# Layer 3 self attention: two norms by single units, and a gate projection in another place

## Chip, cores and metric

The kernel runs on one core of a Trainium2 chip. The metric is the device time of one execution in microseconds (us). A core has five engines that matter here: PE (TensorE, matrix products and transposes), DVE (VectorE), ACT (ScalarE), POOL (GpSimd) and SP, which issues most DMAs. Each engine works through its own queue in order, and engines wait for one another through semaphores.

## What is computed

The program is a network of four layers on 1024 tokens (16 sequences of 64) of 256 channels. The change lies in the self attention of the last layer, a linear attention with convolutions over the sequence around it. Its reference, cut:

```python
x = x + _dwconv(x.transpose(0, 2, 1), cpe1_w, cpe1_b).transpose(0, 2, 1)
shortcut = x
xn = _ln(x, norm1_g, norm1_b)
act_res = silu(xn @ actp_w + actp_b)
xi = xn @ in_w + in_b
xi = silu(_dwconv(xi.transpose(0, 2, 1), dwc_w, dwc_b)).transpose(0, 2, 1)
qk = xi @ qk_w + qk_b
q = elu(qk[..., :c]) + 1.0
k = elu(qk[..., c:]) + 1.0
...
attn = attn + _dwconv(v_bcl, lepe_w, lepe_b).transpose(0, 2, 1)
x = shortcut + attn * act_res @ out_w + out_b
x = x + _dwconv(x.transpose(0, 2, 1), cpe2_w, cpe2_b).transpose(0, 2, 1)
xn2 = _ln(x, norm2_g, norm2_b)
mlp = gelu(xn2 @ fc1_w + fc1_b, approximate=False) @ fc2_w + fc2_b
return x + mlp
```

`_dwconv` is a convolution of three taps along the sequence, one set of taps per channel. `_ln` subtracts the mean over the channels and divides by the root of the variance plus 1e-5, then applies a gain and an offset. `act_res` is called the gate here.

## The kernel before

The method `L3_attn` works on four units (NU) of 256 tokens each. Most tiles are 128 partitions by two halves by 256 elements; a unit lies either feature by token (channels on the partitions, in two halves) or token by feature ("natural"). All eight PSUM banks belong to one pool, `ps`: every matrix product or turn of a unit takes one bank, and a bank is free again when its last reader is done. SBUF tiles come from a pool with four buffers for each tag (`a` to `f`), so that a tag that is used again waits for the readers of what it held.

Instructions that are wrapped in `pin` (and all matrix products and turns, L195 and L199) keep the order of the code on their engine. What isn't wrapped, such as POOL's operations and the builds of the diagonal matrices (L1738), may be placed by the scheduler.

The stages, each a loop over the four units that ends before the next begins:

1. The input is turned to feature by token (L199) and copied by ACT (L1893). `conv` then makes the first convolution: half of the channels on PE as three products with diagonal matrices (`conv_T`) and an evacuation by ACT that adds the bias (L1905), the other half on DVE as three operations (`conv_V`, L1754, L1755 and L1758), here called the taps.
2. `norm`: each unit is turned to natural, `measure` finds mean and variance on DVE (L1813, L1814) and adds 1e-5 (L1816), POOL takes the power -0.5 (L1817), and `normal` subtracts the mean and multiplies on DVE (L1822), one unit behind the measuring.
3. The normalised units are turned back and scaled by gain and offset on ACT (L1829).
4. For each unit, the input projection (bias by DVE, L1919) and then the gate projection (Silu by ACT, L1836, kept in tag `d`).
5. The second convolution with Silu (L1926, L1929).
6. Queries, keys and values: two projections and a turn per unit on PE, exponentials on ACT, elu on DVE (L1939, L1944, L1953), and a third convolution on DVE alone (lepe, six operations of `conv_V`).
7. `products`, `attend` and `gated`, staggered by one unit each: products of keys and values, masked on DVE (L1982, L1986); the attention (L2006 to L2008); the turn back, the sum with lepe (L2020) and the product with the gate on POOL (L2021).
8. The output projection with bias and shortcut on DVE (L2035), for all units; then the third convolution for all units; then `norm` again, which here also adds each natural unit to the residual `x` on DVE (L2049) right after its measuring.
9. Turn, scale, and the two layers of the MLP (`hidden` with Gelu on ACT, L2062, and `output`). The experts of the next stage follow.

An activation function of ACT that isn't in the loaded table set needs a table load first; the trace shows one ahead of the exponentials of stage 6 and one ahead of the Gelus of stage 9.

Of the kernel before, what the change touches and what calls it, by code (L numbers as in the profile page):

```python
# [8 lines left out]
F32 = mybir.dt.float32  # L9
U8 = mybir.dt.uint8  # L10
U32 = mybir.dt.uint32
AF = mybir.ActivationFunctionType
ALU = mybir.AluOpType
# [3 lines left out]
P = 128  # L17
# [156 lines left out]
class Net:  # L174
# [33 lines left out]
    def pv(self, name):  # L208
        o, n = self.pat[name]
        return self.pvec[:, o : o + n]  # L210
# [1529 lines left out]
    def conv_T(self, ps, src, dg):  # L1740


        o = ps.rearrange("p (b s) -> p b s", s=S)
        i = src.rearrange("p (b s) -> p b s", s=S)
        self.mm(o, dg[:, 1, :], i, True, False)
        self.mm(o[:, :, 1:], dg[:, 0, :], i[:, :, : S - 1], False, False)
        self.mm(o[:, :, : S - 1], dg[:, 2, :], i[:, :, 1:], False, True)

    def conv_V(self, out, src, taps, b):

        nc = self.nc
        o = out.rearrange("p (b s) -> p b s", s=S)
        i = src.rearrange("p (b s) -> p b s", s=S)
        self.pinned(nc.vector.tensor_scalar(o, i, taps[1], b, ALU.mult, ALU.add))  # L1754
        self.pinned(nc.vector.scalar_tensor_tensor(  # L1755
            o[:, :, 1:], i[:, :, : S - 1], taps[0], o[:, :, 1:], ALU.mult, ALU.add
        ))
        self.pinned(nc.vector.scalar_tensor_tensor(  # L1758
            o[:, :, : S - 1], i[:, :, 1:], taps[2], o[:, :, : S - 1], ALU.mult, ALU.add
        ))  # L1760
# [4 lines left out]
    def L3_attn(self, w):  # L1765
# [3 lines left out]
        nc, tc = self.nc, self.tc  # L1769
        in_w, actp_w, qk_w, out_w = w  # L1770
        pv = lambda n: self.pv(f"L3_attn_{n}")
        NH, NU, U = 8, 4, 256
        pin = self.pinned
# [4 lines left out]
        with (  # L1778
# [5 lines left out]
            def T(tag):  # L1784
                return wk.tile([P, 2, U], F32, tag=tag, name=tag)
# [4 lines left out]
            def turned(src, at):  # L1790

                ps = bank()
                for i in range(2):
                    for kc in range(2):
                        self.tr(ps[:, i, kc * P : (kc + 1) * P], at(src, i, kc))
                return ps
# [4 lines left out]
            def project(w, src, c0=0):  # L1801
                ps = bank()
                for c in range(2):
                    cols = slice(c0 + c * P, c0 + (c + 1) * P)
                    self.project_T(ps[:, c, :], w, src, cols, slice(None))
                return ps

            def measure(ps):

                mv = small.tile([P, 2, 2], F32, tag="mv", name="mv")  # L1810
                for i in range(2):
                    st = small.tile([P, 6], F32, tag="bst", name="bst")
                    pin(nc.vector.bn_stats(st, ps[:, i, :]))  # L1813
                    pin(nc.vector.bn_aggr(mv[:, i, :], st))  # L1814
                rs = small.tile([P, 2], F32, tag="rs", name="rs")
                pin(nc.vector.tensor_scalar(rs, mv[:, :, 1], 1e-5, None, ALU.add))  # L1816
                nc.gpsimd.tensor_tensor(rs, rs, self.c("pow")[:, 0:1].to_broadcast([P, 2]), ALU.pow)  # L1817
                return ps, mv, rs

            def normal(out, ps, mv, rs):  # L1820
                for i in range(2):
                    pin(nc.vector.tensor_scalar(  # L1822
                        out[:, i, :], ps[:, i, :], mv[:, i, 0:1], rs[:, i : i + 1],
                        ALU.subtract, ALU.mult,
                    ))

            def scaled(out, ps, g, b):
# [6 lines left out]
            def biased(out, ps, fn, b):  # L1834
                for c in range(2):
                    pin(nc.scalar.activation(  # L1836
                        out[:, c, :], ps[:, c, :], fn, bias=b[:, c : c + 1]
                    ))

            def norm(xT, tag, extra=None):  # L1840


                out, due = [], None
                for u in range(NU + 1):
                    now = None
                    if u < NU:
                        ps = turned(xT[u], to_nat)
                        now = measure(ps)
                        if extra is not None:
                            extra(u, ps)  # L1850
                    if due is not None:
                        n = wk.tile([P, 2, U], F32, tag=tag, name=tag)
                        normal(n, *due)
                        out.append(n)
                    due = now
                return out

            self.fixed = True
# [33 lines left out]
                x0T.append(T("a"))  # L1892
                pin(nc.scalar.copy(x0T[u], ps))  # L1893
            self.add_bias(8)
            def conv(out, src, n):
                ps = self.psum(pp, [P, U], "ps")
                self.conv_T(ps, src[:, 0, :], dg[n])
                self.conv_V(out[:, 1, :], src[:, 1, :], taps[n][1], pv(f"{n}_b")[:, 1:2])
                return ps

            x1T = []
            for u in range(NU):
                x1T.append(T("c"))
                ps = conv(x1T[u], x0T[u], "cpe1")
                pin(nc.scalar.activation(  # L1905
                    x1T[u][:, 0, :], ps, AF.Identity, bias=pv("cpe1_b")[:, 0:1]
                ))
            self.diagonals(dg["dwc"], taps["dwc"][0])
            self.diagonals(dg["cpe2"], taps["cpe2"][0])
            n1 = norm(x1T, "a")  # L1910
            xnT = []
            for u in range(NU):
                xnT.append(T("b"))
                scaled(xnT[u], turned(n1[u], to_feat), pv("norm1_g"), pv("norm1_b"))
            act, xi0 = [], []
            for u in range(NU):
                ps = project(in_w, xnT[u])
                xi0.append(T("a"))
                pin(nc.vector.tensor_tensor(xi0[u], ps, wide(pv("in_b")), ALU.add))  # L1919
                act.append(T("d"))  # L1920
                biased(act[u], project(actp_w, xnT[u]), AF.Silu, pv("actp_b"))
            xi = []
            for u in range(NU):
                xi.append(T("e"))
                ps = conv(xi[u], xi0[u], "dwc")
                pin(nc.scalar.activation(  # L1926
                    xi[u][:, 0, :], ps, AF.Silu, bias=pv("dwc_b")[:, 0:1]
                ))
                pin(nc.scalar.activation(xi[u][:, 1, :], xi[u][:, 1, :], AF.Silu))  # L1929

            qT, k, v, lepe = [], [], [], []
            for u in range(NU):
                ps = project(qk_w, xi[u])
                e = sp.tile([P, 2, U], F32, tag="e", name="e")
                biased(e, ps, AF.Exp, pv("qk_b"))
                z = sp.tile([P, 2, U], F32, tag="z", name="z")
                biased(z, ps, AF.Identity, qb1)
                qT.append(T("b"))
                pin(nc.vector.scalar_tensor_tensor(qT[u], e, 1.0, z, ALU.min, ALU.max))  # L1939
                ps = bank()  # L1940
                for i in range(2):
                    self.project_N(ps[:, i, :], xi[u], i, qk_w, slice(D, 2 * D))
                z = sp.tile([P, 2, U], F32, tag="zk", name="zk")
                pin(nc.vector.tensor_tensor(  # L1944
                    z, ps, kb1.unsqueeze(1).to_broadcast([P, 2, D]), ALU.add
                ))
                e = sp.tile([P, 2, U], F32, tag="e", name="e")
                pin(nc.scalar.activation(e, z, AF.Exp, bias=self.c("neg1")))
                ps = turned(xi[u], to_nat)
                v.append(T("a"))  # L1950
                pin(nc.scalar.copy(v[u], ps))
                k.append(T("f"))
                pin(nc.vector.scalar_tensor_tensor(k[u], e, 1.0, z, ALU.min, ALU.max))  # L1953

                lepe.append(self.xn[:, 2 * u : 2 * u + 2, :])
                for c in range(2):
                    self.conv_V(
                        lepe[u][:, c, :], xi[u][:, c, :], taps["lepe"][c],
                        pv("lepe_b")[:, c : c + 1],
                    )  # L1960

            kvm = {}

            def products(u):
# [58 lines left out]
            for n in range(NU + 2):  # L2023
# [3 lines left out]
                    attend(n - 1)  # L2027
                if 0 <= n - 2 < NU:
                    gated(n - 2)
            x2T = []  # L2030
            for u in range(NU):
                ps = project(out_w, y[u])
                x2T.append(T("a"))
                for c in range(2):
# [1 line left out]
                        x2T[u][:, c, :], ps[:, c, :], pv("out_b")[:, c : c + 1], x1T[u][:, c, :],  # L2036
                        ALU.add, ALU.add,
                    ))
            x3T = []
            for u in range(NU):  # L2040
                x3T.append(T("b"))
                ps = conv(x3T[u], x2T[u], "cpe2")
                pin(nc.scalar.activation(
                    x3T[u][:, 0, :], ps, AF.Identity, bias=pv("cpe2_b")[:, 0:1]
                ))

            def add(u, ps):
                xu = self.x[:, 2 * u : 2 * u + 2, :]
                pin(nc.vector.tensor_tensor(xu, ps, xu, ALU.add))  # L2049

            n2 = norm(x3T, "a", add)
            xn2T, hT = [], {}
            for u in range(NU):
                xn2T.append(T("c"))
# [77 lines left out]
```

## Time and profile before

| | |
|---|---|
| median of 3 runs | 3475.49 us (3474.08 to 3479.93) |
| profiled execution | 3481.06 us, span 3479.3 us |
| mean granted PE clock in it | 0.942 of full speed |
| L3_attn, first convolution to the first expert rows | about 3102 to 3257 us of the span |

The profile is one execution as the hardware profiler saw it. Engine rows give busy time; the timeline merges runs of equal instructions and names in brackets how long the engine was idle before, and which engine's instruction ended that. The clock of PE is what the throttle granted, as a share of full speed. A matrix product of 32-bit numbers stands in the trace as two instructions, so 32 instructions are the four products of each of four units. The ends of PE's instructions are modelled, so that starts are the safer reading.

### The profile page before, as it was taken

The numbers are of one execution on the slowest core, as the hardware profiler recorded it, in microseconds if no ns is written. First come the engines' busy times: TensorE is split into PE (matmuls) and PEld (weight loads), VectorE is DVE, ScalarE is ACT, GpSimd is POOL, SyncE is SP. The second block draws the span as 40 slices with busy tenths as digits, with TensorE's granted clock in tenths as the row PEclk, the third lists the DMA queues.
The fourth block names the chain that finished last, engine by engine and source line by source line (L and its number), as shares of the span: only waits on it lengthen the run. The fifth ranks groups of instructions, "written<-read, shape, count | busy, mean of one in ns | idle before, by whom it ended". The sixth has DMA issues, their size and how long they took to land.

```text
span 3479.3 us, 69200 instructions
## 1 busy us (share of the span) xinstructions
PE 3170.8 (91%) x29623; PEld 2365.5 (68%) x29623; DVE 1387.8 (40%) x3702; ACT 1065.1 (31%) x2191; POOL 470.1 (14%) x478
## 2 busy tenths in 40 slices
PE   7999998699899999999998689999987978888798
PEld 4666664499566666666665367777766966767697
DVE  6888885622333333333334862222234010126300
ACT  3555654111112111212111112222221367753111
POOL 2333222222100000000000000000001311110132
PEclk9999998699899999999998699999997979998899
DMA  6333331389011112111139001111114835520297
GB/s 198 103 126 124 94 115 58 122 289 320 17 58 56 57 57 76 38 60 55 57 113 308 15 13 57 57 57 57 38 53 162 273 123 179 187 88 1 107 324 246
DMA packets 178368, 395.12 MB, mean 114 GB/s; under 512 B 11446, under 2 KB 142270, under 8 KB 165214
## 3 DMA queue, kind: packets, MB, share of 16 engines
q1 hardware_dynamic: 165070, 372.81, 31.2%
q0 software_dynamic: 11712, 16.00, 2.3%
q8 instruction: 234, 3.83, 0.5%
q10 hardware_dynamic: 1280, 1.89, 0.2%
q14 instruction: 72, 0.59, 0.1%
HBM read 374.94 MB, written 16.12 MB: 112 GB/s over the span
## 4 chain that ended last, share of the span: by engine, by line
PE 77%; DVE 11%; DMA 5%; issue 5%; POOL 1%; ACT 1%; SPq 0%; POOLq 0%; ACTq 0%; DVEq 0%
PE acc L195 16%; PE pss L195 15%; PE pst L195 13%; PE pst L199 9%; PE pso L195 5%; PE psk L195 5%; PE s L195 4%; PE p L195 4%; DMA l3o<-y,token 3%; PE ps L195 3%; PE psh L195 2%; DVE Sx L447 2%; DVE Sx L470 1%; POOL rs L304 1%; PE py L195 1%
## 5 line engine op out<-in xcount | busy, mean ns | idle before, releaser
L199 PE MATMUL pst<-cst,Sx 128*128 128x128 f32 (+1 forms) x2568 | 377.7, 286 | 42.9 <-DVE Sx L470 14.1
L195 PE MATMUL pss<-ctxT,qk 128*128 128x512 f32 (+1 forms) x1024 | 403.3, 519 | 0.0
L199 PEld LDWEIGHTS pst<-cst,Sx 128*128 128x128 f32 (+1 forms) x2568 | 287.9, 144 | 167.0 <-issue 70.2
L195 PE MATMUL acc<-ctx,PT 128*128 128x256 f32 (+1 forms) x1664 | 374.0, 382 | 0.0
L195 PEld LDWEIGHTS acc<-ctx,PT 128*128 128x128 f32 (+1 forms) x1664 | 314.1, 192 | 40.2
L447 DVE CUSTOM_DVE_ANT_0 Sx<-s,mneg 128x384 f32<-128x384 f32 (+1 forms) x512 | 262.7, 567 | 79.0 <-PE s L195 69.8
L304 POOL TENSOR_TENSOR rs<-rs,cst 128x1 f32<-128x1 f32 x96 | 57.4, 600 | 1602.3 <-DVE rs L303 1495.4
L491 ACT ACTIVATE PT<-pst 128x384 f32<-128x384 f32 x512 | 221.3, 489 | 154.1 <-PE pst L199 152.8
L824 ACT ACTIVATE Pr<-pss 128x512 f32<-128x512 f32 (+1 forms) x512 | 220.4, 523 | 68.8 <-PE pss L195 67.3
L376 ACT ACTIVATE Sx<-Sx,nm 128x1601 f32<-128x1601 f32 x64 | 104.4, 1631 | 432.2 <-DVE nm L630 432.2
L195 PEld LDWEIGHTS pss<-ctxT,qk 128*128 128x128 f32 x1024 | 160.9, 190 | 79.3 <-issue 72.3
L195 PE MATMUL pso<-W,hT 128*128 128x256 f32 x884 | 200.9, 379 | 0.0
L195 PE MATMUL pst<-wst,ctxT 128*128 128x256 f32 (+1 forms) x832 | 183.4, 381 | 0.0
L195 PE MATMUL psk<-ctxT,wst 128*128 128x512 f32 (+1 forms) x512 | 181.8, 513 | 0.8 <-ACT qT L686 0.8
L195 PEld LDWEIGHTS pso<-W,hT 128*128 128x128 f32 x884 | 163.3, 190 | 19.6
L195 PEld LDWEIGHTS pst<-wst,ctxT 128*128 128x128 f32 (+1 forms) x832 | 153.6, 186 | 25.8 <-issue 2.7
L195 PE MATMUL pss<-q,ctxT 32*128 32x128 f32 (+1 forms) x3328 | 151.3, 300 | 16.6 <-issue 13.9
L195 PE MATMUL s<-ctxT,q 32*128 32x384 f32 (+1 forms) x1024 | 160.2, 572 | 6.3 <-DVE mx L447 4.9
L625 DVE TENSOR_SCALAR_CACHE_REDUCE Sx<-pss 128x1024 f32<-128x1024 f32 (+1 forms) x128 | 127.0, 992 | 82.6 <-PE pss L195 82.6
L640 DVE TENSOR_SCALAR Z<-acc,rec 128x256 f32<-128x256 f32 x64 | 31.0, 484 | 322.6 <-PE acc L195 322.6
L195 PEld LDWEIGHTS pss<-q,ctxT 32*128 32x128 f32 (+1 forms) x3328 | 119.4, 194 | 48.5 <-issue 39.5
L195 PEld LDWEIGHTS psk<-ctxT,wst 128*128 128x128 f32 x512 | 88.3, 190 | 93.6 <-issue 92.0
(387 smaller groups left out, 4479.1 us busy)
## 6 DMA issues: line engine op xcount, KB each, us to landing
ctxT<-in_ctxT_dram SPq DMA_DIRECT2D x64, 1601.0 KB
ctx<-in_ctx_dram SPq DMA_DIRECT2D x48, 1536.0 KB
W<-in_L_experts_dram SPq DMA_DIRECT2D x61, 1024.0 KB
W<-in_L_experts_dram SPq DMA_DIRECT2D x23, 1536.0 KB
ctx<-in_ctx_ones_dram SPq DMA_DIRECT2D x16, 1632.0 KB
W<-in_L_experts_dram SPq DMA_DIRECT2D x23, 768.0 KB
W<-in_L_experts_dram SPq DMA_DIRECT2D x15, 1028.0 KB
m<-in_mask_dram SPq DMA_DIRECT2D x32, 100.1 KB
```

Of the source, the lines that this page charges most:

```text
L195: self.pinned(self.nc.tensor.matmul(out, lhsT, rhs, start=start, stop=stop))
L199: self.pinned(self.nc.tensor.transpose(out, in_, self.ident[:n, :n]))
L304: nc.gpsimd.tensor_tensor(rs, rs, self.c("pow")[:, 0:1], ALU.pow)
L376: nc.scalar.activation(Sx, Sx, AF.Exp, bias=bias, scale=scale, accum_out=total)
L447: self.pinned(nc.vector.tensor_tensor_reduce(out=Sx[:, j, :n], in0=ps[j][:, :n], in1=st["mneg"][:, o : o + n], op0=ALU.add, op1=ALU.max, s ...
L470: self.pinned(nc.vector.tensor_scalar(Sj[j], Sj[j], m[:, j : j + 1], None, ALU.subtract))
L491: self.pinned(nc.scalar.activation(PT, ps, AF.Exp))
L625: nc.vector.tensor_scalar(Sx[:, o : o + n], ps[:, :n], HD**-0.5, None, ALU.mult, ALU.max, accum_out=mx[:, h : h + 1],)
L640: nc.vector.tensor_scalar(Z, acc, rec, None, ALU.mult)
L824: nc.scalar.activation(st["Pr"][:kn, g : g + n, j, :], ps[j][:kn, :n, :], AF.Silu)
```

## The change

Four things change in `L3_attn`:

- `norm` gets a function that makes the convolution of one unit, and calls it unit by unit: convolve, turn and measure unit u, normalise unit u - 1. Before, all four convolutions were made ahead of it. In `first` and `third`, PE's part, DVE's part and ACT's evacuation of one unit stand together.
- `normal` runs on ACT: it computes x times the inverse deviation plus minus mean times the inverse deviation. For that, DVE negates the mean (one more operation of 128 by 2), and POOL makes one more product.
- The gate projection moves from stage 4 to a place behind stage 6; its tiles take tag `b`, the queries tag `d`.
- In stage 8, DVE's part of the third convolution follows each unit's output projection. The additions to the residual come after the whole norm, which holds the natural units' banks until then.

```diff
-                rs = small.tile([P, 2], F32, tag="rs", name="rs")
-                pin(nc.vector.tensor_scalar(rs, mv[:, :, 1], 1e-5, None, ALU.add))
-                nc.gpsimd.tensor_tensor(rs, rs, self.c("pow")[:, 0:1].to_broadcast([P, 2]), ALU.pow)
-                return ps, mv, rs
+                rs = small.tile([P, 2, 2], F32, tag="rs", name="rs")
+                pin(nc.vector.tensor_scalar(rs[:, 0, :], mv[:, :, 1], 1e-5, None, ALU.add))
+                pin(nc.vector.tensor_scalar(rs[:, 1, :], mv[:, :, 0], -1.0, None, ALU.mult))
+                nc.gpsimd.tensor_tensor(
+                    rs[:, 0, :], rs[:, 0, :], self.c("pow")[:, 0:1].to_broadcast([P, 2]), ALU.pow
+                )
+                nc.gpsimd.tensor_tensor(rs[:, 1, :], rs[:, 1, :], rs[:, 0, :], ALU.mult)
+                return ps, rs
...
-                    pin(nc.vector.tensor_scalar(
-                        out[:, i, :], ps[:, i, :], mv[:, i, 0:1], rs[:, i : i + 1],
-                        ALU.subtract, ALU.mult,
+                    pin(nc.scalar.activation(
+                        out[:, i, :], ps[:, i, :], AF.Identity, bias=rs[:, 1, i : i + 1],
+                        scale=rs[:, 0, i : i + 1],
                     ))
...
-            def norm(xT, tag, extra=None):
+            def norm(conv, tag, extra=None):
...
-                        ps = turned(xT[u], to_nat)
+                        ps = turned(conv(u), to_nat)
                         now = measure(ps)
-                        if extra is not None:
-                            extra(u, ps)
+                        nat.append(ps)
                     if due is not None:
                         n = wk.tile([P, 2, U], F32, tag=tag, name=tag)
                         normal(n, *due)
                         out.append(n)
                     due = now
+                if extra is not None:
+                    for u in range(NU):
+                        extra(u, nat[u])
...
-            for u in range(NU):
+            def first(u):
                 x1T.append(T("c"))
-                ps = conv(x1T[u], x0T[u], "cpe1")
+                ps = conv_T(x0T[u], "cpe1")
+                conv_V(x1T[u], x0T[u], "cpe1")
                 pin(nc.scalar.activation(
                     x1T[u][:, 0, :], ps, AF.Identity, bias=pv("cpe1_b")[:, 0:1]
                 ))
+                return x1T[u]
+
+            n1 = norm(first, "a")
             self.diagonals(dg["dwc"], taps["dwc"][0])
             self.diagonals(dg["cpe2"], taps["cpe2"][0])
-            n1 = norm(x1T, "a")
...
-                act.append(T("d"))
-                biased(act[u], project(actp_w, xnT[u]), AF.Silu, pv("actp_b"))
...
+            act = []
+            for u in range(NU):
+                ps = project(actp_w, xnT[u])
+                act.append(T("b"))
+                biased(act[u], ps, AF.Silu, pv("actp_b"))
             kvm = {}
...
-            x3T = []
-            for u in range(NU):
-                x3T.append(T("b"))
-                ps = conv(x3T[u], x2T[u], "cpe2")
+                x3T.append(T("d"))
+                conv_V(x3T[u], x2T[u], "cpe2")
+
+            def third(u):
+                ps = conv_T(x2T[u], "cpe2")
                 pin(nc.scalar.activation(
                     x3T[u][:, 0, :], ps, AF.Identity, bias=pv("cpe2_b")[:, 0:1]
                 ))
+                return x3T[u]
...
-            n2 = norm(x3T, "a", add)
+            n2 = norm(third, "a", add)
```

More of the change, by code (lines that the diff above doesn't have):

```diff
@@ L1814, in measure, with normal @@
                     pin(nc.vector.bn_aggr(mv[:, i, :], st))
-                rs = small.tile([P, 2], F32, tag="rs", name="rs")
-                pin(nc.vector.tensor_scalar(rs, mv[:, :, 1], 1e-5, None, ALU.add))
-                nc.gpsimd.tensor_tensor(rs, rs, self.c("pow")[:, 0:1].to_broadcast([P, 2]), ALU.pow)
-                return ps, mv, rs
-            def normal(out, ps, mv, rs):
+                rs = small.tile([P, 2, 2], F32, tag="rs", name="rs")
[6 more added lines that the diff above has]
+                return ps, rs
+            def normal(out, ps, rs):
                 for i in range(2):
-                    pin(nc.vector.tensor_scalar(
-                        out[:, i, :], ps[:, i, :], mv[:, i, 0:1], rs[:, i : i + 1],
-                        ALU.subtract, ALU.mult,
+                    pin(nc.scalar.activation(
+                        out[:, i, :], ps[:, i, :], AF.Identity, bias=rs[:, 1, i : i + 1],
+                        scale=rs[:, 0, i : i + 1],
                     ))
@@ L1838, in biased @@
                     ))
-            def norm(xT, tag, extra=None):
-                out, due = [], None
+            def norm(conv, tag, extra=None):
+                out, nat, due = [], [], None
                 for u in range(NU + 1):
@@ L1894, in L3_attn, with conv_V, conv_T @@
             self.add_bias(8)
-            def conv(out, src, n):
+            def conv_V(out, src, n):
+                self.conv_V(out[:, 1, :], src[:, 1, :], taps[n][1], pv(f"{n}_b")[:, 1:2])
+            def conv_T(src, n):
                 ps = self.psum(pp, [P, U], "ps")
                 self.conv_T(ps, src[:, 0, :], dg[n])
-                self.conv_V(out[:, 1, :], src[:, 1, :], taps[n][1], pv(f"{n}_b")[:, 1:2])
                 return ps
             x1T = []
-            for u in range(NU):
+            def first(u):
                 x1T.append(T("c"))
-                ps = conv(x1T[u], x0T[u], "cpe1")
+                ps = conv_T(x0T[u], "cpe1")
+                conv_V(x1T[u], x0T[u], "cpe1")
                 pin(nc.scalar.activation(
@@ L1914, in L3_attn @@
                 scaled(xnT[u], turned(n1[u], to_feat), pv("norm1_g"), pv("norm1_b"))
-            act, xi0 = [], []
+            xi0 = []
             for u in range(NU):
@@ L1924, in L3_attn @@
                 xi.append(T("e"))
-                ps = conv(xi[u], xi0[u], "dwc")
+                ps = conv_T(xi0[u], "dwc")
+                conv_V(xi[u], xi0[u], "dwc")
                 pin(nc.scalar.activation(
@@ L1937, in L3_attn @@
                 biased(z, ps, AF.Identity, qb1)
-                qT.append(T("b"))
+                qT.append(T("d"))
                 pin(nc.vector.scalar_tensor_tensor(qT[u], e, 1.0, z, ALU.min, ALU.max))
@@ L2029, in L3_attn @@
                     gated(n - 2)
-            x2T = []
+            x2T, x3T = [], []
             for u in range(NU):
```

## The prediction

> **What bounds the kernel now.** I read the page first, its busy times:
>
> ```profile
> PE 3170.8 (91%) x29623; PEld 2365.5 (68%) x29623; DVE 1387.8 (40%) x3702; ACT 1065.1 (31%) x2191; POOL 470.1 (14%) x478
> ```
>
> PE is by far the busiest engine, so the question in any stage is what PE waits for. The operations of the changed method lie between 3099 and 3256 us of the span, so I read the timeline of PE there, then that of VectorE (DVE) at PE's gaps, the waits, and last the stretches' granted clock. Columns of a timeline: start, length, engine, line, operation, count, and in brackets the idle time before.
>
> PE's timeline, in the order of the steps below:
>
> ```profile
> 3101.83 5.29 PE L195 MATMUL ps<-a,dgs 128*128 128x256 f32 x24
> 3106.96 1.91 PE L199 MATMUL ps<-cst,c 128*128 128x128 f32 x16
> 3110.86 0.91 PE L199 MATMUL ps<-cst,a 128*128 128x128 f32 x4 [1.99 <-DVE a L1822]
> 3113.05 1.26 PE L199 MATMUL ps<-cst,a 128*128 128x128 f32 x4 [1.28 <-DVE a L1822]
> 3115.24 2.17 PE L199 MATMUL ps<-cst,a 128*128 128x128 f32 x8 [0.93 <-DVE a L1822]
> 3117.20 15.28 PE L195 MATMUL ps<-b,wst 128*128 128x256 f32 x64
> 3132.31 5.29 PE L195 MATMUL ps<-a,dgs 128*128 128x256 f32 x24
> ...
> 3164.57 2.08 PE L195 MATMUL ps<-kvm,b 128*64 128x136 f32 x16 [7.23 <-DVE kvm L1986]
> ...
> 3195.80 1.27 PE L199 MATMUL ps<-cst,a 128*128 128x128 f32 x4 [3.76 <-DVE a L1822]
> 3198.59 1.26 PE L199 MATMUL ps<-cst,a 128*128 128x128 f32 x4 [1.52 <-DVE a L1822]
> 3201.37 2.17 PE L199 MATMUL ps<-cst,a 128*128 128x128 f32 x8 [1.52 <-DVE a L1822]
> ```
>
> PE waits three times: in the first norm (4.2 us in three pieces), before the attention (7.23), in the second norm (6.8). Each time DVE is behind. Between 3132 and 3164 the chain of waits runs through DVE and ScalarE (ACT), 5.46 us a unit, while PE runs ahead and ends at 3157.3.
>
> VectorE's timeline at both ends of that stretch, and ACT's last work there:
>
> ```profile
> 3131.40 0.40 DVE L1754 TENSOR_SCALAR e<-a,pvec 128x256 f32<-128x256 f32 x1
> ...
> 3163.10 1.28 DVE L1982 TENSOR_TENSOR kvm<-ps,cst 128x512 f32<-128x512 f32 x2
> ```
> ```profile
> 3138.43 1.28 ACT L1836 ACT_TABLE_LOAD   x1
> ...
> 3159.65 0.56 ACT L1951 COPY a<-ps 128x512 f32<-128x512 f32 x1
> ```
>
> Windows of 3.41 us (length, PE busy and count, clock granted, DMA share, GB/s):
>
> ```profile
> 3109.66:3113.07 3.41, 0.87 (x5) 0.99 0.00 0
> 3113.07:3116.49 3.42, 2.50 (x9) 0.50 0.00 0
> 3116.49:3119.90 3.41, 3.41 (x12) 0.51 0.02 5
> 3157.45:3160.86 3.41, 0.00 (x0) 0.50 0.00 0
> 3164.27:3167.69 3.42, 3.12 (x26) 0.51 0.02 5
> 3201.82:3205.23 3.41, 3.41 (x13) 0.51 0.00 0
> ```
>
> Each idle stretch costs twice: PE then works at half clock until a full window has passed. The 64 projections took 15.28 us where 32 warm ones take 7.07: 1.1 us lost.
>
> **What the Trainium skill says.** "TensorE: Matmul & The Clock Gate", Part 1, has a free-running window of 3413 ns, half clock after an idle one and full clock after a busy one. The trace agrees: all changes above fall on one grid of 3.41 us. It does not say where between idle and busy the line runs; in this trace, of fifteen full-speed windows with 52 to 60% busy, nine were followed by full and six by half speed. "PSUM — Partial Sum Buffer", Engine vs sequencer instructions, calls ScalarE's, VectorE's and GpSimd's queues strict FIFO: an ACT instruction that waits holds all behind it; in the trace ACT starts its work in the order of the code throughout the method. "ScalarE: Activation LUTs", What ACT_TABLE_LOAD costs, gives 1283 ns for a load and about 1380 for the drain; the trace shows 1.28 and no gap after it. "GPSIMD Engine Reference", Specifications, says that POOL shares SBUF interfaces with DVE: a 128x128 DVE operation took 0.75 us beside POOL's 128x256 add (3101.63), but a pair took 0.47 beside a power (3100.23), so I charge the small POOL operations nothing on DVE.
>
> **Step 1, the first norm (loss 2.5).** Before, all convolutions end on PE at 3107.12 and the projections start at 3117.41. After, unit u+1's DVE taps come behind unit u's measuring, and that waits for unit u's turn on PE, which waits for its taps. The loop on DVE: measuring 1.30 (3107.59 to 3108.89) plus 0.09 for the added TENSOR_SCALAR, taps 1.35 (a quarter of 5.4), 0.14 to PE, three turns of four at 0.15, 0.05 back: 3.38 a unit. The first measuring starts at 3101.99 + 1.28 (convolution) + 0.51 (ACT) + 0.14 + 0.60 + 0.05 = 3104.6, the fourth at 3114.7, done 3116.1. Then POOL's power 0.70 and the new product. No row shows a 128x2 product; the bounds are 0.10 (the 128x1 memsets) and 0.70 (the power); I take 0.3, since 128x256 and 128x512 products or adds (0.75 and 1.27) leave about 0.23 as fixed part. ACT's two normalising operations take 1.02 as a pair (the same form at L1829), so they end at 3118.3. The scaling of unit 0 is queued behind them on ACT, 0.56 and a wait of 0.14 for its first half: projections start at 3119.3, 2.0 later than now. PE is busy 1.9 of 3.4 us in the loop, 56%, in the doubtful band: 0.5 more, as a share of the 1.4 that half speed would cost. The six diagonal builds moved behind the norm (0.27 each) fall into DVE's waits of 0.6 a unit.
>
> **Step 2, gate projection and its ACT work leave the stretch (gain 6.1).** Now: 3117.41 to 3138.43 (ACT free for the table load), 21.0. After: 32 projections 7.07, 1.2 for a cold start as now; then DVE is last, not PE: 0.05, the last bias add 0.61, four units of taps 5.50 (3131.40 to 3136.90), 0.04, the last Silu 0.41, together 6.6 (PE's convolutions need 5.6). Sum 14.9. So the keys' stretch starts 6.1 - 2.5 = 3.6 earlier. Inside it nothing changes: DVE and ACT set the 5.46 a unit.
>
> **Step 3, the gate projection in PE's gap (0).** PE ends the keys' work 3153.1 - 3.6 = 3149.5 or before; 7.07 of projections end by 3156.5; the first products 2.2, 3158.7. The eight PSUM banks: the four gate banks are freed by ACT's Silus, which wait on ACT behind the last key's exponent and copy (3160.2 - 3.6 = 3156.6), an added table load 1.28, then 0.84 for the first unit and 0.73 each: 3158.7, 3159.5. The second products need these two banks and end at about 3161.0. The attention would wait for DVE's masks until 3164.57 - 3.6 = 3161.0 anyway. Cost 0; with the page's drain on top, 1.4. What is late next is DVE again. POOL's gating first needs a gate at 3168 or later.
>
> **Step 4, PE warm at the attention (gain 0.6).** The first 16 attention matmuls took 2.08 against 1.15 later, the next 16 products 1.64 against 1.16: 1.4 on PE. DVE, 91% busy there, idled 0.64 and 0.19 for PE; I take 0.6 of the 0.8.
>
> **Step 5, the second norm (gain 2.6).** DVE now ends its taps at 3191.44. After, each unit's 0.88 (two adds) and 1.36 (taps) go side by side with the output projections, 2.27 a unit from 3180.03: done at 3189.1. PE's loop from 3185.1: convolution 1.28, ACT 0.51, 0.14, turns 0.6. ACT's queue decides from the third unit: unit 0 is measured by 3190.5, through POOL 3191.65, normalised on ACT until 3192.7, and only behind this comes unit 2's convolution evacuation; so unit 2 is turned at 3193.85, unit 3 at 3196.35, measured 3197.8, through POOL 3199.0, normalised 3200.0, scaled behind it; the hidden layer starts at 3200.9 against 3203.54. The residual adds (0.6 each), now last on DVE, hold two PSUM banks until 3199.1, just in time. The cold start there, 0.8 now, I leave as it is. Behind it PE bounds the rest of the method, and the routing of the experts starts from its last row, so a shift carries to the end.
>
> **Sum.** -2.5 + 6.1 + 0 + 0.6 + 2.6 = 6.8 us. It is made on the execution with span 3479.3 and time 3481.06, which lies 5.6 above the median shown; the difference goes on the median: 3475.49 - 6.8 = 3468.7. Bounds of the unknowns: product -0.2/+0.4 twice, drain +1.4, clock -2 to +3.
>
> **Rivals.** (a) Half clock takes the gain back: the first loop falls to half speed (0.9 over my allowance), the projections start cold in an unlucky window (1.3 more), the second loop loses 1.2 and the hidden layer 0.9. Gain 2.5, 3473.0. For it: the 56%. Against: the second loop is 60 to 75% busy at first. (b) All stays warm and the windows fall well: 0.6 less in step 1, 1.2 saved in the projections, 0.2 more in step 4, 0.8 more at the hidden layer, and the allowance of 0.5 back: gain 10.1, 3465.4. (c) Slower: half speed from the second unit of both loops makes PE itself the loop's bound: convolution 2.57, ACT and waits 0.65, turns 1.2, so 4.4 a unit against 3.4 and 2.5. That is 2.6 over my allowance and 1.0 more at the projections in the first, 4.5 and 0.9 in the second: 9.0 lost against 6.8 gained, 3477.7. It decides when both loops go cold by their second unit; more than 0.2% needs the drain and a bank wait in step 3 as well, or a mechanism that I don't see.
>
> **How the numbers follow.** About 0.2%, 7 us, is what a measurement of this kernel can tell from no change. Chances: forecast 0.46 (3465 to 3472), (a) 0.22, (b) 0.20, (c) 0.12. Over half of the forecast's own spread and all of (b) lie at 7 us or more: faster 0.48; slower by 0.2%, most of (c) with what I overlook: 0.09; the rest 0.43. Range 3462 to 3476: it leaves out the end of (b) and (c).
>
> **What would show it.** Right: PE's 7.23 us gap gone, gate projections in it, the first 16 attention matmuls near 1.15; projections starting near 3119 with DVE as the loop's bound; one more table load; the hidden layer some 7 us earlier. Wrong: half clock through the first loop; a PE wait for ACT's Silu before the second products; PE waiting for residual adds in the second norm; the third unit's evacuation not held by the normalising.

## The result

| | before | changed |
|---|---|---|
| median of 20 runs each | 3473.98 us (3464.96 to 3484.77) | 3464.36 us (3455.90 to 3474.02) |
| profiled execution | 3481.06 us, span 3479.3 | 3462.45 us, span 3460.7 |

The changed kernel takes 0.9975 of the time before (95% interval 0.9964 to 0.9986), or 8.7 us less (4.9 to 12.5). 6.8 were forecast. The median is inside the forecast's range of 3462 to 3476, but 4.3 us under its single number of 3468.7. Of these, 1.5 come from the base: 20 runs put the kernel before at 3473.98, the three runs shown earlier at 3475.49. The interval also holds the 10.1 us of rival (b), so the times alone do not choose between the forecast and (b).

The two profiled spans differ by 18.6 us, and most of that isn't the change. The first product with a diagonal matrix, where the changed code begins, starts at 3101.83 in the one and at 3090.37 in the other: 11.5 us arise in earlier stages, whose code is the same, and I did not look for their cause. So all stage times below are counted from that product (the origin), each in its own execution:

| from the origin to, us | before | changed | difference |
|---|---|---|---|
| projections start | 15.37 | 17.02 | +1.65 |
| table load ahead of the exponentials | 36.60 | 32.58 | -4.02 |
| attention's first product | 62.74 | 58.72 | -4.02 |
| output projection | 76.20 | 72.32 | -3.88 |
| hidden layer's first product | 101.51 | 94.64 | -6.87 |
| last product of the method | 157.83 | 150.18 | -7.65 |
| end of the span | 377.47 | 370.33 | -7.14 |

The page's busy times of the changed kernel, then its PE timeline in the order of the steps:

```profile
PE 3158.9 (91%) x29623; PEld 2352.3 (68%) x29623; DVE 1381.7 (40%) x3694; ACT 1073.6 (31%) x2208; POOL 473.7 (14%) x486
```
```profile
3095.93 0.55 PE L199 MATMUL ps<-cst,c 128*128 128x128 f32 x3 [0.72 <-DVE c L1758]
...
3099.37 0.55 PE L199 MATMUL ps<-cst,c 128*128 128x128 f32 x3 [0.72 <-DVE c L1758]
...
3106.48 1.00 PE L199 MATMUL ps<-cst,a 128*128 128x128 f32 x4 [1.81 <-ACT a L1826]
3107.39 8.88 PE L195 MATMUL ps<-b,wst 128*128 128x256 f32 x32
3116.11 5.29 PE L195 MATMUL ps<-a,dgs 128*128 128x256 f32 x24
...
3136.81 7.07 PE L195 MATMUL ps<-b,wst 128*128 128x256 f32 x32
...
3146.95 1.16 PE L195 MATMUL ps<-a,f 64*128 64x128 f32 x14 [0.58 <-ACT b L1840]
3148.04 1.05 PE L195 MATMUL ps<-cst,f 128*128 128x2 f32 x8
3149.09 2.08 PE L195 MATMUL ps<-kvm,d 128*64 128x136 f32 x16
3151.11 1.77 PE L195 MATMUL ps<-a,f 64*128 64x128 f32 x16
...
3177.74 0.66 PE L199 MATMUL ps<-cst,d 128*128 128x128 f32 x4 [1.68 <-ACT d L2060]
...
3184.09 1.00 PE L199 MATMUL ps<-cst,a 128*128 128x128 f32 x4 [1.50 <-ACT a L1826]
3185.01 14.11 PE L195 MATMUL ps<-c,ctxT 128*128 128x256 f32 x64
```

The reader is to see three things. The turns of units 1 and 2 in the first norm are 3.44 us apart, each after a wait for DVE's taps. The 7.23 us gap ahead of the attention is gone: the gate projection fills it, and 0.58 of waiting for a Silu is left. But the attention's first 16 products take 2.08 us as before: the gap has gone and the slow start has not. In the second norm the turn of the third unit waits 1.68 us for ACT, where the other three wait 0.56 or 0.57.

The windows (length, PE busy and count, clock, DMA share, GB/s) of the changed kernel, laid on the changes of this execution's clock to within 0.1 us; the first is in the first norm, the next two around the start of the projections, the last two around the start of the attention:

```profile
3096.01:3099.42 3.41, 2.13 (x11) 1.00 0.00 0
3104.57:3107.98 3.41, 1.47 (x8) 1.00 0.00 0
3107.98:3111.40 3.42, 3.42 (x10) 0.51 0.00 0
3145.53:3148.94 3.41, 2.83 (x28) 1.00 0.00 0
3148.94:3152.36 3.42, 3.42 (x30) 0.51 0.00 0
```

A window with 2.13 us of busy PE keeps the clock, one with 1.47 loses it. The fourth loses it too, although PE was busy for 2.83 of its 3.41 us. That is the one thing in the trace that the prediction's picture doesn't explain, and half of the experiments turn on it.

### The profile page after: what moved, and what is told of

Read it like the earlier page. It is cut to its first block, busy times and chain, and to the rows that moved or that the text cites. A ratio compares the mean times of both kernels' runs of the same rounds, so it can differ in the third digit from the quotient of the medians.

```text
span 3460.7 us, 69219 instructions
## 1 busy us (share of the span) xinstructions
PE 3158.9 (91%) x29623; PEld 2352.3 (68%) x29623; DVE 1381.7 (40%) x3694; ACT 1073.6 (31%) x2208; POOL 473.7 (14%) x486
## 4 chain that ended last, share of the span: by engine, by line
PE 78%; DVE 12%; issue 4%; DMA 3%; POOL 1%; ACT 1%; SPq 0%; POOLq 0%; ACTq 0%; DVEq 0%
PE acc L195 16%; PE pss L195 15%; PE pst L195 13%; PE pst L199 9%; PE pso L195 6%; PE psk L195 5%; PE p L195 4%; PE s L195 4%; PE psh L195 3%; PE ps L195 2%; DVE Sx L447 2%; DMA l3o<-y,token 1%; DVE Sx L470 1%; POOL rs L304 1%; PE py L195 1%
## 5 line engine op out<-in xcount | busy, mean ns | idle before, releaser
L195 PE MATMUL pss<-q,ctxT 32*128 32x128 f32 (+1 forms) x3328 | 149.2, 296 | 16.3 <-issue 13.5
L726 DVE TENSOR_TENSOR v<-pst,bvec 128x512 f32<-128x512 f32 (+1 forms) x112 | 73.0, 652 | 196.2 <-PE pst L195 196.2
```

The source lines that it names most:

```text
L195: self.pinned(self.nc.tensor.matmul(out, lhsT, rhs, start=start, stop=stop))
L726: nc.vector.tensor_tensor(o, ps[:kn, :n, :], bv[:kn].to_broadcast([kn, n, D]), ALU.add)
```

## Experiments

My theory after the traces: the change is a sum of parts (move of the gate projection, first norm, second norm) that can be read off the marks, plus a clock effect in the attention's stage that was not understood. The rival: the parts hang together, or the clock is just noise. All kernels were profiled once and timed (6 to 22 runs) against the kernel before; ratios are to it. It was timed anew with each group of kernels, with medians of 3476.26, 3471.64 and 3476.01, so times of different groups are compared by ratios. "Marks" are four starts counted from the origin: projections, attention, output projection, hidden layer; "the stage" is the time from attention to output projection.

**The move alone.** The kernel before, with the gate projection behind the keys' work and the tags adapted:

```diff
-                act.append(T("d"))
-                biased(act[u], project(actp_w, xnT[u]), AF.Silu, pv("actp_b"))
...
+            act = []
+            for u in range(NU):
+                ps = project(actp_w, xnT[u])
+                act.append(T("b"))
+                biased(act[u], ps, AF.Silu, pv("actp_b"))
             kvm = {}
```

> The kernel before with the gate projection moved and nothing else. Marks count from the first diagonal product of the first convolution: projections start at 15.4, the attention's first product at 62.7, the output projection at 76.2, the hidden layer at 101.5 in the kernel before, and at 17.0, 58.7, 72.3 and 94.6 in the changed one. Theory (the parts add up, and this move alone shortens the way from projections to attention by 5.6): 15.4, 57.1, 70.6 and 96, so 5.5 us faster than before. Rival (the norms and the move are worth something only together, since the gap closes from both sides): less than 3 us faster.

Measured: ratio 0.9986 (0.9976 to 0.9997), 4.9 us faster. Marks 15.37, 57.10, 76.33, 101.64. The attention comes 5.64 earlier, as the theory says, and in the profiled execution all of it is lost again before the output projection: 19.2 us for a stage that took 13.5. The timeline of this stage (`cst,f` with 128x2 are the sums of the keys, two columns wide) and its windows, laid on the changes of the clock:

```profile
3153.68 1.87 PE L195 MATMUL ps<-cst,f 128*128 128x2 f32 x8
3155.47 2.08 PE L195 MATMUL ps<-kvm,d 128*64 128x136 f32 x16
...
3159.49 1.86 PE L195 MATMUL ps<-cst,f 128*128 128x2 f32 x8
...
3166.35 1.86 PE L195 MATMUL ps<-cst,f 128*128 128x2 f32 x8
...
3171.20 2.08 PE L195 MATMUL ps<-kvm,d 128*64 128x136 f32 x16
```
```profile
3149.95:3153.36 3.41, 2.88 (x36) 1.00 0.00 0
3153.36:3156.78 3.42, 3.42 (x24) 0.50 0.00 0
3156.78:3160.19 3.41, 3.41 (x28) 0.50 0.02 5
3160.19:3163.60 3.41, 3.41 (x24) 0.50 0.00 0
3163.60:3167.02 3.42, 3.42 (x24) 0.50 0.00 0
3167.02:3170.43 3.41, 3.41 (x24) 0.50 0.00 0
3170.43:3173.84 3.41, 3.41 (x23) 0.50 0.00 0
```

From 3153.36 on PE is busy without a hole, and five full windows in a row do not bring the clock back: busy time in the profile isn't what the throttle counts. Each of the five holds between 0.67 and 1.87 us of the two-column sums. The sixth, from 3170.43, holds none, and after it the clock is full.

**The norms alone.** The changed kernel with the gate projection back in its old place.

> The changed kernel with the gate projection back beside the input projection. Theory: the first norm costs 1.7, the second gives 3.0 and a warm hidden layer 0.8: marks 17.0, 64.4 to 65, 78 to 78.5 and 100.5, so 1 to 2 us faster than before. Rival (the norms carry most of the gain): 4 us or more faster.

Measured: 0.9995 (0.9987 to 1.0003); marks 17.03, 64.91, 78.77, 101.09, last product 156.64 against 157.83. The theory holds: the two norms together are worth 1.2 us in the trace and cannot be told from nothing in the times. By the ratios the move gives 4.9 us and the norms 1.7, 6.6 together against 8.7 of the changed kernel, which is within their intervals. The marks of these two traces do not add up like that (101.64 and 101.09 against 94.64), because of the 5.8 us that the move's trace lost at half clock.

**Normalising back on VectorE.** The changed kernel with `measure` and `normal` as they were:

```diff
-                    pin(nc.scalar.activation(
-                        out[:, i, :], ps[:, i, :], AF.Identity, bias=rs[:, 1, i : i + 1],
-                        scale=rs[:, 0, i : i + 1],
+                    pin(nc.vector.tensor_scalar(
+                        out[:, i, :], ps[:, i, :], mv[:, i, 0:1], rs[:, i : i + 1],
+                        ALU.subtract, ALU.mult,
                     ))
```

> The changed kernel with the normalising back on VectorE, one unit behind the measuring, without the negated mean and POOL's product. Theory: in the first norm VectorE bounds the loop, so three more pairs of 0.9 lengthen it: projections at 19.4 against 17.0. In the second norm VectorE has room and ACT's queue no longer holds the third unit's evacuation: from output projection to hidden layer 21 against 22.3. In sum about 1 us slower than the changed kernel. Rival (normalising on ACT is no gain since it stands in front of the evacuations in both norms): projections at 17.0 or earlier, and faster than the changed kernel.

Measured: 0.9977 (0.9968 to 0.9986), against 0.9975 of the changed kernel. Projections at 18.58, so ACT's normalising saves 1.56 in the first norm (2.4 were expected from three longer rounds of the loop; only two got longer, 4.27 and 4.28 us against 3.44). From output projection to hidden layer 20.82 against 22.32: in the second norm it costs 1.50. PE's turns there come 2.5 us apart, with the convolution's evacuation as the only wait; the third unit's:

```profile
3186.78 0.66 PE L199 MATMUL ps<-cst,d 128*128 128x128 f32 x4 [0.56 <-ACT d L2056]
```

So the hold in ACT's queue, an older unit's normalising in front of the next unit's evacuation, is shown. The two cancel: that it is ACT that normalises is worth nothing in sum.

**Additions back in the loop.**

```diff
-                        nat.append(ps)
+                        if extra is not None:
+                            extra(u, ps)
```

> The changed kernel with the residual additions back in the second norm's loop, after each measuring. Theory (PE's turns and ACT's queue bound that loop, and VectorE has 1.7 and 1.0 us of waits in it): from output projection to hidden layer 22.3 as in the changed kernel, within 0.2. Rival (VectorE bounds it): 1.2 to 1.8 us later.

Measured: 0.9976 (0.9966 to 0.9986); output projection to hidden layer 22.31 against 22.32. Putting off the additions bought nothing: DVE has waits for PE in this loop that take them.

**Wide sums.** `products` multiplies the keys by a matrix of two columns to sum them. Each of those products is now 128 columns wide, so that every sum comes out 64 times:

```diff
-                pks = self.psum(pp, [P, 2, 4], "ps")
+                pks = self.psum(pp, [P, 2, 4, 64], "ps")
...
-                            pks[:, c, 2 * i : 2 * i + 2], k[u][:, i, c * P : (c + 1) * P],
-                            self.c("half"),
+                            pks[:, c, 2 * i : 2 * i + 2, :], k[u][:, i, c * P : (c + 1) * P],
+                            half64,
```

Here `half64` is `self.c("half")` with each column broadcast 64 times, and `pks[:, :, :, 0]` is used.

> The changed kernel with the key sums' products 128 columns wide instead of 2 (each sum repeated 64 times, the first is used). Theory (the throttle counts columns streamed, and the 2-column products are idle to it though the profile shows PE busy): the window before the attention counts as busy, the attention's first 16 products take 1.15 to 1.3 us instead of 2.08 and the next 16 about 1.2 instead of 1.77; output projection 0.3 to 0.8 us earlier. Rival (the 0.58 us wait for ACT's Silu, or the products of half height, bring the half clock): still near 2.08 and 1.77, nothing gained.

Measured: 0.9961 (0.9944 to 0.9977). The stage's timeline and two of its windows:

```profile
3147.14 1.16 PE L195 MATMUL ps<-a,f 64*128 64x128 f32 x14 [0.48 <-ACT b L1840]
3148.23 1.16 PE L195 MATMUL ps<-cst,f 128*128 128x128 f32 x8
3149.32 1.15 PE L195 MATMUL ps<-kvm,d 128*64 128x136 f32 x16
```
```profile
3145.72:3149.13 3.41, 2.93 (x29) 1.00 0.00 0
3149.13:3152.55 3.42, 3.42 (x43) 1.00 0.02 5
```

Eight of the wide instructions take 1.16 us, eight of the narrow ones took 1.05, with the same number of loads of stationary matrices; the attention now starts at full speed, and the stage takes 12.27 us instead of 13.60. The windows lie almost as in the changed kernel (the attention begins 0.2 us behind an edge here, 0.1 there), and the window ahead of the attention is as busy as there (2.93 us against 2.83), so neither the grid nor the busy time makes the difference. The wait for the Silu (0.48) and the products of half height are still there, so neither brings the half clock without the narrow sums.

The gain does not reach the end of the method in this trace. The hidden layer starts 1.06 earlier than in the changed kernel, but its first 64 instructions run partly at half clock (15.24 us against 14.11), and the last product ends at 150.27 against 150.18.

**Wide sums on the two others.** The same edit on the kernel before and on the move alone.

> The kernel before with the key sums 128 columns wide and nothing else. Theory (the wide sums are worth something only through the clock; here PE idles 7 us ahead of the attention and starts it at half clock whatever the width): the first 16 attention products 2.08, from attention to output projection 13.0 to 13.5 as before, the time within 2 us of before. Rival (wider products are faster or slower by themselves, or end the cold stretch earlier): more than 1 us of difference in that stage.

Measured: 0.9998 (0.9990 to 1.0006); the first 16 products 2.08, the stage 13.80 against 13.46. As expected, width alone is no gain where PE idles ahead of the stage.

> The kernel before with the gate projection moved and the key sums 128 columns wide. Theory (the move's 5.6 us were eaten in the profile of the move alone by half clock through the whole attention stage, 19.2 us against 13.5, and the narrow sums kept the clock from rising): attention at 57.1, output projection at 69.4 to 69.8, hidden layer at 94.7 to 95.3, so 6 to 7 us faster than before. Rival (the stage is long for another reason, as POOL's gating or ACT's later Silus): output projection at 73 or later.

Measured: 0.9970 (0.9962 to 0.9977), 10.4 us faster. Marks 15.38, 56.98, 69.25, 94.56: the stage takes 12.27 us instead of the 19.23 of the move alone, and the attention starts at full speed:

```profile
3141.51 1.15 PE L195 MATMUL ps<-kvm,d 128*64 128x136 f32 x16
```

By the ratios the wide sums give 5.5 us over the move alone, with intervals that just meet (0.9962 to 0.9977, 0.9976 to 0.9997). In the traces the move of the gate projection is worth 6.9 us on its own if the clock is kept, and with the wide sums it needs no change of the norms to reach the changed kernel's hidden layer (94.64).

**Convolutions one unit ahead.** In the changed kernel's `norm`, for both norms:

```diff
+                made = [conv(0)]
                 for u in range(NU + 1):
                     now = None
                     if u < NU:
-                        ps = turned(conv(u), to_nat)
+                        if u + 1 < NU:
+                            made.append(conv(u + 1))
+                        ps = turned(made[u], to_nat)
```

> The changed kernel with each unit's convolution issued one unit ahead of the turn, in both norms. Theory (the turn's way over PE and back, 0.64 us a unit, stands on VectorE's chain in the first norm, and in the second norm ACT's normalising stands in front of the next convolution's evacuation; both go away): projections start at 13.9 instead of 17.0, from output projection to hidden layer 19.2 instead of 22.3, the method 6 us shorter but for the clock in the attention's stage. Rival (PE's order or ACT's queue only moves the wait): less than 1 us in each norm.

Measured: 0.9961 (0.9948 to 0.9974). Projections at 13.97; from output projection to hidden layer 19.79 against 22.32, where 19.2 was expected. The last turns of the first norm and all turns of the second:

```profile
3101.12 1.45 PE L195 MATMUL ps<-a,dgs 128*128 128x256 f32 x6
3102.40 0.60 PE L199 MATMUL ps<-cst,c 128*128 128x128 f32 x4
3103.93 0.33 PE L199 MATMUL ps<-cst,c 128*128 128x128 f32 x1 [0.92 <-ACT c L1918]
3105.17 0.88 PE L199 MATMUL ps<-cst,c 128*128 128x128 f32 x3 [0.92 <-DVE c L1758]
...
3176.49 0.60 PE L199 MATMUL ps<-cst,d 128*128 128x128 f32 x4
...
3178.21 0.60 PE L199 MATMUL ps<-cst,d 128*128 128x128 f32 x4
...
3179.93 0.60 PE L199 MATMUL ps<-cst,d 128*128 128x128 f32 x4
3182.06 0.66 PE L199 MATMUL ps<-cst,d 128*128 128x128 f32 x4 [1.53 <-ACT d L2063]
```

The first three turns follow their convolutions without a wait. The last one still meets an evacuation behind a normalising in both norms. In the second norm this is what is left of the hold (1.53); in the first, VectorE's taps come later still (the second 0.92), so there VectorE alone sets the end. The attention's stage took 16.1 us here (first 16 products 2.08, next 2.08), and the hidden layer's first 64 instructions 15.77, so some of the gain was lost to the clock.

**Both.** Convolutions ahead and wide sums.

> The changed kernel with the convolutions one unit ahead and the key sums 128 columns wide. Theory: both gains add, projections at 13.9, the attention's stage at full clock (attention to output projection 12.3), output projection to hidden layer 19.2: the method 7.5 us shorter than the changed kernel, some 15 us under the kernel before. Rival (an earlier projection start meets a colder PE, or the earlier attention meets ACT's Silus): 4 us or less.

Measured: 0.9952 (0.9939 to 0.9966), 16.7 us faster than before. Marks 14.21, 55.52, 67.79, 87.59, last product 143.14: 7.0 us less than the changed kernel and 14.7 less than the kernel before. The projections met half clock for longer in this execution (table load at 29.35, against 27.84 with the convolutions ahead alone).

**The first half as one pipeline.** With both edits, one loop over steps s in place of four loops:

```diff
+            first(0)
+            for s in range(NU + 4):
+                if s + 1 < NU:
+                    first(s + 1)
+                if s < NU:
+                    m1.append(measure(turned(x1T[s], to_nat)))
+                if 0 <= s - 1 < NU:
+                    n1.append(T("a"))
+                    normal(n1[s - 1], *m1[s - 1])
+                if 0 <= s - 2 < NU:
+                    xnT.append(T("b"))
+                    scaled(xnT[s - 2], turned(n1[s - 2], to_feat), pv("norm1_g"), pv("norm1_b"))
+                if 0 <= s - 3 < NU:
+                    ps = project(in_w, xnT[s - 3])
+                    xi0.append(T("f"))
+                    pin(nc.vector.tensor_tensor(xi0[s - 3], ps, wide(pv("in_b")), ALU.add))
+                if 0 <= s - 4 < NU:
...
```

The last branch is the second convolution with its Silus.

> As the one with both edits, and the first half pipelined over the units: in one loop unit s + 1 is convolved, s turned and measured, s - 1 normalised, s - 2 turned back and scaled, s - 3 projected, s - 4 convolved for the second time. Theory (behind the first norm all engines wait for the last unit's power, normalising, turn and scaling while three units could be projected): ACT reaches the table load of the exponentials at 22 to 25 instead of 32.6 (29.5 with the convolutions ahead alone), so 5 us or more faster again. Rival (VectorE's order puts the bias additions in front of waits that PE sets, PE loses clock in a thinner loop): 29 or later.

Measured: 0.9941 (0.9926 to 0.9955), 20.5 us faster than before and the lowest ratio of all, though its interval overlaps that of the version without the pipeline. Table load at 25.25, hidden layer at 83.48, last product at 140.63. This is less than expected: 22 to 25 for the table load, and 5 us or more over the version without the pipeline. The hidden layer comes 4.1 earlier than there, and 2.5 are left at the last product, because the hidden layer's first 64 instructions took 15.71 us instead of 14.10. PE's timeline in it:

```profile
3104.06 0.55 PE L199 MATMUL ps<-cst,c 128*128 128x128 f32 x3 [0.91 <-DVE c L1758]
3104.71 1.00 PE L199 MATMUL ps<-cst,a 128*128 128x128 f32 x4
3105.62 2.02 PE L195 MATMUL ps<-b,wst 128*128 128x256 f32 x8
3107.47 0.60 PE L199 MATMUL ps<-cst,a 128*128 128x128 f32 x4
3107.91 2.02 PE L195 MATMUL ps<-b,wst 128*128 128x256 f32 x8
```

The first unit is projected one turn behind the last unit's own, where PE used to wait for power, normalising, turn and scaling of the last unit.

## Why the prediction was right, and where it wasn't

**Step 1, first norm: the mechanism right, too dear by 0.85.** 2.5 were charged (2.0 and 0.5 for the clock), 1.65 were lost. The loop's period is 3.44 us against 3.38, with VectorE waiting for PE and PE for VectorE's taps, as worked out. VectorE's measuring of the second unit, then POOL's work for the third and the last:

```profile
3096.51 0.43 DVE L1813 BATCH_NORM_STATS2 bst<-ps 128x6 f32<-128x256 f32 x1 [0.64 <-PE ps L199]
```
```profile
3101.42 0.86 POOL L1818 TENSOR_TENSOR rs<-rs,cst 128x2 f32<-128x2 f32 x1 [2.05 <-DVE rs L1817]
3102.35 0.45 POOL L1821 TENSOR_TENSOR rs<-rs 128x2 f32<-128x2 f32 x1
3104.86 0.70 POOL L1818 TENSOR_TENSOR rs<-rs,cst 128x2 f32<-128x2 f32 x1 [2.05 <-DVE rs L1817]
3105.63 0.20 POOL L1821 TENSOR_TENSOR rs<-rs 128x2 f32<-128x2 f32 x1
```

The last unit's product took 0.20, not the 0.3 estimated. The rest of the 2.0 is a slip in the sum: 3118.3 and the two terms named after it, 0.56 and 0.14, make 3119.0 and not 3119.3, and 3119.0 is 1.6 behind 3117.41. The 0.5 for the clock was not needed in the loop: it stayed at full clock at 62% busy (the prediction put it at 56%). Of rival (a) only its second part came, and in part: the projections started colder than allowed for, as step 2 shows.

**Step 2, the move: the mechanism right, 0.4 less.** 5.67 us against 6.1: the projections' cold start cost 1.8 (8.88 against 7.07) where I had left it at 1.2. That VectorE's taps would be last and not PE was right: PE's convolutions end at 3121.4, ACT's last Silu, held by the taps, at 3122.95. Steps 1 and 2 together: 4.02 earlier against 3.6.

**Step 3, the gap: right.** The bank wait of 0.58 came where step 3 put it, between the two products. The prediction's closing list names a PE wait for ACT's Silu at this place as a sign of being wrong; its own step implies the wait, and it cost nothing. The second products end at 3149.09 and the masks at 3149.03, the tie that was worked out: the lead of 4.02 is passed on whole. The table load took 1.28 us, and the first Silu began 0.02 after it (3144.76 and 3146.06), so the drain of about 1380 ns that the Trainium skill's page "ScalarE: Activation LUTs", What ACT_TABLE_LOAD costs, adds does not show.

**Step 4, a warm start of the attention: wrong.** +0.6 was predicted, -0.14 came. The step that failed is its premise that PE would be warm because the gap was filled. The runs show in its place that filling the gap with instructions isn't enough. With two-column sums in front of the attention, half clock follows: its first 16 products took 2.07 or 2.08 us in all five traces with the gate projection in the gap. With the same sums 128 columns wide they took 1.15 in all four. I could have seen it in the trace of before, whose window ahead of the gap was full and still was followed by half clock:

```profile
3154.03:3157.45 3.42, 3.30 (x38) 0.99 0.00 0
3157.45:3160.86 3.41, 0.00 (x0) 0.50 0.00 0
```

The Trainium skill's page "TensorE: Matmul & The Clock Gate", Part 1, speaks of how busy PE has been; the measurement says that the profile's busy time isn't that. What is counted instead, columns, multiplications or something else, the runs do not show: only widths of 2 and 128 were tried. Nor did I see the size of it: I allowed 3 us for all effects of the clock together, while the move alone lost 5.8 us in this stage in its profiled execution.

**Step 5, second norm: right, 0.4 more.** 2.99 us against 2.6, and 0.77 at the hidden layer, whose first 64 instructions ran warm (14.11 against 14.88), which I had left at nothing. ACT's hold of the third unit was there, 1.68 us. The additions fitted in, as worked out, and the runs say that they would have fitted in the loop too.

**The sum.** 6.8 were forecast; the trace has 7.65 at the method's last product and 7.14 at the end, the times 8.7 with an interval of 4.9 to 12.5. It came out right partly by terms that cancel: steps 1 and 5 better than charged by 0.85 and 0.4 and the warm hidden layer by 0.8, steps 2 and 4 worse by 0.4 and 0.7. It is also luck that the changed kernel's profiled execution lost only one window to step 4's mistake; the move alone lost six. Of rival (b) the warm hidden layer came, the warm projections did not. Rival (c), slower, needed both loops at half clock; neither was.

How much the attention's stage loses depends on where the edges of the clock's windows fall. In the five traces with narrow sums and the gate projection in the gap, the clock falls at a window's edge 0.06 us behind the attention's first product, or 0.09, 1.29, 1.39 and 2.11 ahead of it, and the stage takes 13.7, 13.6, 16.1, 16.1 and 19.2 us. All nine full windows at half clock that held 0.67 us or more of the narrow sums were followed by another one; the five that held 0.45 or less were followed by full clock. So the changed kernel's 13.6 is the good case. How often each case comes over many executions stays open; I did not count it.

## What to carry to other kernels

When a gap on PE is filled, look at what kind of work stands in the last clock window ahead of the critical products: products of two columns filled the timeline here and left the clock to fall, and widening them to 128 columns cost 0.1 us for eight instructions. Then look at what the next stage does with the time: in several runs here part of the gain was lost again to half clock in the hidden layer. A loop that goes convolve, turn, measure for one unit after another puts the way to PE and back on VectorE's chain; issue the producer one unit ahead, and check each engine's queue for an instruction of an older unit standing in front of the next unit's evacuation. Read stage times from an origin inside the same execution before two profiled spans are compared.

## What the hardware showed that I had not expected

- The throttle does not go by the profile's busy time. In the move alone, five full windows in a row (3.41 us busy of 3.41) at half clock were followed by half clock again; with 128 columns instead of 2 in one kind of product the same stage ran at full clock from start to end, 12.27 instead of 19.23 us.
- POOL is slowed by VectorE, not only the reverse. The power on 128x2 took 0.86 us and the product 0.45 beside VectorE's taps, 0.70 and 0.20 with VectorE idle (the four POOL lines above). VectorE's statistics did not slow it: in the second norm the power at 3175.29 took 0.70 beside them.
